# Attention block in float32: scores in half tiles on two single PSUM banks, four banks for the staggered Strassen products, and the residual sum on VectorE

## The chip, the core and the metric

The kernel runs on one core of a Trainium2 chip. A core has a matmul engine (TensorE, PE in the profile; its weight loads are shown as PEld), VectorE (DVE), ScalarE (ACT), GpSimd (POOL) and SyncE (SP), which here issues nearly all DMAs. Each engine works through its own queue of instructions in order and waits on semaphores of the others. Matmuls write into PSUM, which has eight banks of 128 x 512 float32; VectorE and ScalarE read them, GpSimd can't. The metric is the device time of one execution in microseconds; a lower time is better. Executions of this kernel before agree within 0.1% (3429.11 to 3431.4 us).

## The reference

For each of 16 images x of 512 channels by 1024 positions (all float32):

```python
xn = group_norm(x, 8 groups, eps=1e-5) * gamma + beta
q, k, v = split(qkv_w @ xn + qkv_b, 3)           # 4 heads of 128 channels
attn = softmax(q^T k * 128 ** -0.5, axis=keys)    # per head, 1024 x 1024
out = proj_w @ (v attn^T) + proj_b
return x + out
```

## The kernel before

**Attention.** The loop runs over steps s; a step is one image b, one head h and one block j of 128 keys, so a head has 8 steps (NB) and an image 32. `scores(s)` multiplies the key block with all 1024 queries in two matmuls of 512 into one tile of two banks (pool `ps_s`, two such tiles), takes the exponential of the 1024 columns in one ScalarE instruction (L626) and adds the result to the head's running total on VectorE (L629, L631). `weighted_sum(s)` multiplies values by exponentials into `po`, one tile of two banks (pool `ps_o`) in which all 8 steps of a head accumulate; after the last step ScalarE copies it out in one instruction (L671). `denominators` reduces the total on VectorE and sends the reciprocal through memory to all partitions; `divide` (L674) applies it two steps into the next head. In the program's order a step is: scores of s, then the step's part of the plan, then (at a head's first step) the denominators of the head before, then the weighted sum of s - 1.

**Products with the weights.** Queries, keys, values and the projection are computed by Strassen's method: seven products for a 2 x 2 block product. `strassen` makes seven units of work, in the order of ORDER = 1, 2, 6, 5, 7, 4, 3. A set of units uses two PSUM banks: x holds products 1, 6, 7 and 4, which accumulate on one another, with a copy by ScalarE after each (`kept_copy`, L398, and L496 or L579); y holds product 2, and then, as a new tile, products 5 and 3; VectorE adds the copies to them when it reads them out (L498, L581). Pool `ps_a` has one bank for x and one for y, so a new y must wait until the old one is read.

For queries and keys of two heads (`qk_groups`) and for the projection (`proj_groups`) the method is applied at two levels (`two_levels`): the seven outer products are done in four groups of (1, 5), (2, 6), (7, 4) and (3), and each group runs the seven inner products for its members side by side, with 256 columns each. The first unit of a group (`prepare`) fetches the weights and forms the four inner sums t1 to t4 on VectorE (L468); the last one calls `combine`, which adds up the outer level (L511 to L518) and calls `finish`. For queries and keys `finish` adds the bias (L532); for the projection it loads the residual x into a tile y (SP, L593), adds it on GpSimd to one of the two addends (L602, `eng`), then on VectorE adds bias and the other addend (L603) and stores the result. The values (`v_units`) need one level, in two sets.

**The plan.** While a head's attention runs, its plan puts other work into the eight steps (`plan_head`, `spread`): in h = 0 queries and keys of the image's second pair of heads; in h = 1 the projection of the image before, and the load, statistics and normalisation of the next image; in h = 2 the values of the next image; in h = 3 queries and keys of its first pair. Units of one group follow those of the group before without overlap. For the first image, and for the last image's projection after the loop, there is no attention to run beside: there `staggered` runs two sets against each other, with a lag of 1 or 4 units, and the second set uses a tile of `ps_s` as its two banks (`spare`), other pools' tiles for the sums (`room`) and for one result (`r3`).

The order of instructions on each engine isn't only the program's: a scheduler places instructions at compile time, by the program's order as priority, as soon as its own reckoning has their inputs ready and their tiles free, and it assigns PSUM and SBUF buffers. In the trace the halves of a weighted sum stand between products. What an engine does at run time follows that fixed order.

Of the kernel before, what the change touches and what calls it, by code (L numbers as in the profile page):

```python
# [16 lines left out]
P = 128  # L17
# [130 lines left out]
def fast_path(ctx, tc, x, sources, out, consts, flag, dims):  # L148
# [30 lines left out]
    ps_a = ctx.enter_context(tc.tile_pool(name="ps_a", bufs=1, space=PSUM))  # L179
# [202 lines left out]
    def strassen(name, mm, out_, spare=False, width=HALF):  # L382
# [4 lines left out]
        def bank(which):  # L387
            if spare:
                if "both" not in t:
                    t["both"] = ps_s.tile([P, N], F32, tag="s", name=f"{name}_spare")  # L390
                return t["both"][:, ts("xy".index(which), HALF)]
            return ps_a.tile([P, HALF], F32, tag=which, name=f"{name}_{which}")
# [41 lines left out]
    def two_levels(name, site, b, blocks, finish, spare=(), room=None, r3=None):  # L434

# [8 lines left out]
        def group_units(g):  # L444
# [4 lines left out]
            def prepare():  # L449
                have["w"] = group_weights(site, g, b == 0 and site != "proj")  # L450
                if g == 3:
                    R[g] = r3() if r3 else rpool.tile(
                        [P, 2, 2, HALF], F32, tag="r0", name=f"{name}_r3"
                    )
                else:
                    R[g] = rpool.tile([P, 2, 2, HALF], F32, tag=f"r{g}", name=f"{name}_r{g}")
                sums = ("t1", "t2", "t3", "t4")
                if g in spare:
                    for m, t in zip(sums, room(f"{name}_{g}")):
                        have[m] = t.rearrange("p (i q) -> p i q", q=Q)  # L460
                else:
                    for m in sums:
                        have[m] = tpool.tile(
                            [P, 2, Q], F32, tag=f"in_{m}", name=f"{name}_{g}_{m}"
                        )
                for i, p in enumerate(group):
                    def put(o, a, c):
                        nc.vector.tensor_sub(have[o][:, i, :], inner(i, a), inner(i, c))  # L468
                    put("t1", "b12", "b11")
                    put("t2", "b22", "t1")  # L470
                    put("t3", "t2", "b11")
                    put("t4", "b21", "t2")
# [27 lines left out]
            units = strassen(f"{name}_{g}", mm, out_, g in spare, n * Q)  # L500
            first = units[0]
# [250 lines left out]
    def run(units):  # L752
        for u in units:
            u()
# [188 lines left out]
```

## Time and profile before

| What | Value |
|---|---|
| median of 3 runs | 3430.12 us |
| the profiled execution, and its span | 3429.16 us, 3427.4 us |
| before the first score matmul | 70.5 us |
| after the last weighted sum | 50.0 us |
| PE, PEld, DVE, ACT, POOL busy | 96%, 58%, 72%, 34%, 6% |
| granted TensorE clock, mean | 0.994 |
| DMA | 104 GB/s over the span |

A profile shows one execution. Busy time is what an engine spent in instructions; matmul rows are pipelined, and their ends are modelled, so that the distance between two starts says more than a busy share. In a row of a timeline stand the start, the length, the engine, the line, the operation, the tiles (result <- inputs) and the number of instructions merged; in brackets the idle time ahead of it and what ended it. In a row of the view of waits stand the waiting and the awaited instruction, then the total in us, how many times, and the longest.

### The profile page before, as it was taken

To read this page: it belongs to the slowest core of one execution; us is meant where nothing else is said; L and a number is where in the kernel's file an instruction comes from. 1 tells how busy PE (TensorE), PEld (TensorE's weight loads), DVE (VectorE), ACT (ScalarE), POOL (GpSimd) and SP (SyncE) were. 2 spreads that over 40 slices of the span, in tenths; PEclk is the share of its full clock that TensorE was granted. 3 is DMA by queue.
4 is the path that set the end of the run, shared out by engine and by line. 5 is a ranking of instruction groups with operands and counts; after the bars stand their busy time and mean duration, and the time that the engine had idled before them with its cause. 6 is when DMAs were issued, how large, how long until landed. Compare 5 with 4: busy or idle time off the path is not lost.

```text
span 3427.4 us, 30729 instructions
## 1 busy us (share of the span) xinstructions
PE 3282.7 (96%) x10708; PEld 1985.4 (58%) x10708; DVE 2473.8 (72%) x4305; ACT 1172.2 (34%) x1602; POOL 190.9 (6%) x140
## 2 busy tenths in 40 slices
PE   7999999999999999999999999999999999999997
PEld 6565555655556555565555656555565555655654
DVE  8858577675776858668586785867758677586776
ACT  2423334233333333333333333333333333333332
POOL 0000101000010000101001010010100101001010
PEclk9999999999999999999999999999999999999998
DMA  5323333233332333333233332323323233233232
GB/s 167 127 77 123 104 102 104 93 109 102 101 111 88 110 111 108 106 103 109 85 109 107 107 111 81 119 92 109 116 74 119 95 109 118 76 112 111 81 109 79
DMA packets 114018, 357.37 MB, mean 104 GB/s; under 512 B 15424, under 2 KB 27200, under 8 KB 113856
## 3 DMA queue, kind: packets, MB, share of 16 engines
q1 hardware_dynamic: 112848, 354.27, 30.8%
q8 instruction: 87, 1.43, 0.2%
q10 hardware_dynamic: 1008, 1.06, 0.1%
q14 instruction: 75, 0.61, 0.1%
HBM read 310.00 MB, written 45.29 MB: 104 GB/s over the span
## 4 chain that ended last, share of the span: by engine, by line
PE 70%; DVE 12%; DMA 11%; ACT 3%; issue 2%; POOL 2%; SPq 1%; POOLq 0%; ACTq 0%; DVEq 0%
PE po L665 19%; PE s L621 18%; PE qk_x L483 9%; PE qk_y L483 7%; PE v_x L561 5%; PE pp_x L483 4%; PE v_y L561 4%; DMA rinv<-row 3%; DMA w_v<-kept_v 3%; PE pp_y L483 3%; DVE y L603 2%; DVE tot L631 2%; POOL pp_r L602 2%; ACT x L232 1%; DMA y<-in_x 1%
## 5 line engine op out<-in xcount | busy, mean ns | idle before, releaser
L665 PE MATMUL po<-p,v 128*128 128x512 f32 x2048 | 1018.7, 593 | 15.0 <-ACT o L671 15.0
L626 ACT ACTIVATE p<-s 128x1024 f32<-128x1024 f32 x512 | 523.5, 1023 | 1364.7 <-PE s L621 1285.2
L621 PE MATMUL s<-qk,qk 128*128 128x512 f32 x2048 | 979.7, 596 | 0.0
L631 DVE TENSOR_TENSOR tot<-tot,p 128x1024 f32<-128x1024 f32 x384 | 468.4, 1220 | 365.0 <-ACT p L626 363.4
L621 PEld LDWEIGHTS s<-qk,qk 128*128 128x128 f32 x2048 | 387.3, 191 | 376.0 <-issue 355.1
L665 PEld LDWEIGHTS po<-p,v 128*128 128x128 f32 x2048 | 387.5, 190 | 162.9 <-issue 100.4
L483 PE MATMUL qk_x<-qk_t,w 128*128 128x256 f32 x1326 | 364.6, 391 | 0.3 <-ACT qk_u L398 0.3
L483 PEld LDWEIGHTS qk_x<-qk_t,w 128*128 128x128 f32 x1326 | 238.3, 189 | 176.0 <-ACT qk_u L398 79.3
L602 POOL TENSOR_TENSOR pp_r<-pp_r,y 128x512 f32<-128x512 f32 x120 | 173.0, 1451 | 2927.0 <-ACT pp_r L496 2686.4
L498 DVE TENSOR_TENSOR qk_r<-qk_y,qk_u 128x512 f32<-128x512 f32 x252 | 156.0, 619 | 46.0 <-PE qk_y L483 45.8
L398 ACT COPY qk_u<-qk_x 128x512 f32<-128x512 f32 x252 | 133.8, 531 | 154.3 <-PE qk_x L483 153.7
L483 PE MATMUL pp_x<-pp_t,w_proj 128*128 128x256 f32 x654 | 181.8, 395 | 0.0
L561 PE MATMUL v_y<-w_v,x 128*128 128x256 f32 x720 | 172.4, 379 | 0.0
L561 PE MATMUL v_x<-w_v,xt 128*128 128x256 f32 x720 | 171.4, 381 | 0.0
L483 PEld LDWEIGHTS pp_x<-pp_t,w_proj 128*128 128x128 f32 x654 | 115.8, 190 | 90.8 <-ACT pp_u L398 38.2
L561 PEld LDWEIGHTS v_y<-w_v,x 128*128 128x128 f32 x720 | 136.7, 190 | 49.8 <-issue 28.1
L561 PEld LDWEIGHTS v_x<-w_v,xt 128*128 128x128 f32 x720 | 135.6, 190 | 40.7 <-issue 14.8
L483 PE MATMUL qk_y<-x,w 128*128 128x256 f32 x504 | 143.8, 387 | 15.3 <-DVE qk_r L498 14.5
L483 PEld LDWEIGHTS qk_y<-x,w 128*128 128x128 f32 x504 | 90.7, 189 | 88.5 <-DVE qk_r L498 68.0
L532 DVE SCALAR_TENSOR_TENSOR qk<-qk_r,qkb_sb,qk_r 128x512 f32<-128x512 f32 x190 | 136.3, 746 | 1.1
L483 PE MATMUL qk_y<-qk_t,w 128*128 128x256 f32 x442 | 122.6, 394 | 3.1 <-DVE qk_r L498 3.1
L483 PEld LDWEIGHTS qk_y<-qk_t,w 128*128 128x128 f32 x442 | 78.8, 189 | 77.2 <-DVE qk_r L498 57.4
(202 smaller groups left out, 3523.5 us busy)
## 6 DMA issues: line engine op xcount, KB each, us to landing
w<-kept SPq DMA_DIRECT2D x90, 896.0 KB, 4.7
w_v<-kept_v SPq DMA_DIRECT2D x60, 768.0 KB, 4.4
w_proj<-kept_proj SPq DMA_DIRECT2D x48, 896.0 KB, 4.7
rinv<-row SPq DMA_DIRECT2D x64, 512.0 KB, 3.7
y<-in_x SPq DMA_DIRECT2D x128, 256.0 KB, 3.6
out_y<-y SPq DMA_DIRECT2D x128, 256.0 KB, 2.3
x<-in_x SPq DMA_DIRECT2D x62, 512.0 KB, 4.1
w<-kept SPq DMA_DIRECT2D x30, 448.0 KB, 3.3
```

Of the source, the lines that this page charges most:

```text
L232: nc.scalar.activation(t, t, AF.Identity, bias=beta_sb[:, i], scale=sc[:, i])
L398: nc.scalar.copy(t[n][:, :width], t["x"][:, :width])
L483: nc.tensor.matmul(acc[:, ts(i, Q)], have["w"][:, i, SLOTS[an], :], inner(i, bn), start=(first and i == 0), stop=True, skip_group_check=True,)
L498: nc.vector.tensor_add(dst, view(a), view(c))
L532: nc.vector.scalar_tensor_tensor(st[b, h][:, ts(half, HALF)], a[:, r, :], qkb_sb[:, i : i + 1], c[:, r, :], ALU.add, ALU.add,)
L561: nc.tensor.matmul(acc[:, ts(g, HC)], xb[b][bn][k][:, ts(2 * jj + g, P)], wi[:, k, :], start=(first and g == 0 and k == 0), stop=(k == KC ...
L602: eng.tensor_add(c[:, r, :], c[:, r, :], t)
L603: nc.vector.scalar_tensor_tensor(t, a[:, r, :], projb_sb[:, o : o + 1], c[:, r, :], ALU.add, ALU.add)
L621: nc.tensor.matmul(sc[:, ts(half, HALF)], ks[b, h][:, ts(j, P)], qs[b, h][:, ts(half, HALF)], start=True, stop=True,)
L626: nc.scalar.activation(ps[s], sc, AF.Exp, scale=SCALE)
L631: nc.vector.tensor_add(tot[b, h], tot[b, h], ps[s])
L665: nc.tensor.matmul(po[b, h][:, ts(half, HALF)], vs[b, h // 2][:, h % 2, j, :], p[:, ts(half, HALF)], start=(j == 0), stop=(j == NB - 1),)
```

## The change

PSUM has eight banks in both. Before: two tiles of two banks for scores, one of two for `po`, one bank each for x and y. After: two tiles of one bank for scores, one of two for `po`, two banks each for x and y.

- `scores` and `weighted_sum` take a half as argument. A step is now: (at a head's first step) denominators of the head before; then for each half of 512 queries the scores of s with their exponential, the weighted sum of s - 1, and half of the step's part of the plan. The total is added after the second half, in one instruction as before. `po` is copied out in halves.
- The groups of units are always staggered: group g starts at position 0, 4, 8 or 14 (0, 4, 10 for three groups), in the plan as well as in prologue and tail. `spare`, `room` and `r3` are gone.
- `prepare` is taken apart: weights, t1 and t2 come with product 1, t3 with product 2, t4 with product 6. The result tiles of a group take turns in three buffers (g % 3).
- The residual is added on VectorE, in the other order: bias, first addend and residual in one instruction, then the second addend.
- The load of the next image, its statistics and its normalisation come one step earlier in h = 1.

```diff
-    ps_a = ctx.enter_context(tc.tile_pool(name="ps_a", bufs=1, space=PSUM))
+    ps_a = ctx.enter_context(tc.tile_pool(name="ps_a", bufs=2, space=PSUM))
...
-            def prepare():
+            def weights():
+                R[g] = rpool.tile([P, 2, 2, HALF], F32, tag=f"r{g % 3}", name=f"{name}_r{g}")
                 have["w"] = group_weights(site, g, b == 0 and site != "proj")
...
+            def inner_sum(m):
+                have[m] = tpool.tile([P, 2, Q], F32, tag=f"in_{m}", name=f"{name}_{g}_{m}")
+                a, c = {
+                    "t1": ("b12", "b11"), "t2": ("b22", "t1"), "t3": ("t2", "b11"),
+                    "t4": ("b21", "t2"),
+                }[m]
+                for i in range(n):
+                    nc.vector.tensor_sub(have[m][:, i, :], inner(i, a), inner(i, c))
...
-            units = strassen(f"{name}_{g}", mm, out_, g in spare, n * Q)
-            first = units[0]
-            units[0] = lambda: (prepare(), first())
-            last = units[-1]
-            units[-1] = lambda: (last(), combine(g))
-            return units
+            p1, p2, p6, p5, p7, p4, p3 = strassen(f"{name}_{g}", mm, out_, n * Q)
+            return [
+                lambda: (weights(), inner_sum("t1"), inner_sum("t2"), p1()),
+                lambda: (inner_sum("t3"), p2()), lambda: (inner_sum("t4"), p6()),
+                p5, p7, p4, lambda: (p3(), combine(g)),
+            ]
...
-                eng.tensor_add(c[:, r, :], c[:, r, :], t)
                 nc.vector.scalar_tensor_tensor(
-                    t, a[:, r, :], projb_sb[:, o : o + 1], c[:, r, :], ALU.add, ALU.add
+                    t, a[:, r, :], projb_sb[:, o : o + 1], t, ALU.add, ALU.add
                 )
+                nc.vector.tensor_add(t, t, c[:, r, :])
...
-    def scores(s):
+    def scores(s, half):
         b, h, j = where(s)
-        sc = ps_s.tile([P, N], F32, tag="s", name=f"s_{s}")
-        for half in range(NH2):
-            nc.tensor.matmul(
-                sc[:, ts(half, HALF)], ks[b, h][:, ts(j, P)], qs[b, h][:, ts(half, HALF)],
-                start=True, stop=True,
-            )
-        ps[s] = ppool.tile([P, N], F32, tag="p", name=f"p_{s}")
-        nc.scalar.activation(ps[s], sc, AF.Exp, scale=SCALE)
+        sc = ps_s.tile([P, HALF], F32, tag="s", name=f"s_{s}_{half}")
+        nc.tensor.matmul(
+            sc, ks[b, h][:, ts(j, P)], qs[b, h][:, ts(half, HALF)], start=True, stop=True
+        )
+        if half == 0:
+            ps[s] = ppool.tile([P, N], F32, tag="p", name=f"p_{s}")
+        nc.scalar.activation(ps[s][:, ts(half, HALF)], sc, AF.Exp, scale=SCALE)
+        if half == 0 or j == 0:
+            return
...
         if j == NB - 1:
-            os_[b, h] = opool.tile([P, N], F32, tag="o", name=f"o_{b}_{h}")
-            last_eviction[b] = nc.scalar.copy(os_[b, h], po.pop((b, h)))
+            if half == 0:
+                os_[b, h] = opool.tile([P, N], F32, tag="o", name=f"o_{b}_{h}")
+            last_eviction[b] = nc.scalar.copy(os_[b, h][:, i], po[b, h][:, i])
...
+    def staggered(lists):
+        starts = (0, 4, 8, 14)[: len(lists)] if len(lists) != 3 else (0, 4, 10)
+        at = [(a + i, g, u) for g, (a, us) in enumerate(zip(starts, lists))
+              for i, u in enumerate(us)]
+        return [u for _, _, u in sorted(at, key=lambda t: t[:2])]
...
-            spread(plan, sum(qk_groups(b, 1), []), 0, NB)
+            spread(plan, staggered(qk_groups(b, 1)), 0, NB)
...
-                plan[1].append(lambda: load_x(b + 1))
-                spread(plan, [lambda c=c: stats_chunk(b + 1, c) for c in range(NCC)], 3, 7)
-                plan[6].append(lambda: stats_group(b + 1))
-                plan[7] += [lambda c=c: normalise(b + 1, c) for c in range(NCC)]
+                plan[0].append(lambda: load_x(b + 1))
+                spread(plan, [lambda c=c: stats_chunk(b + 1, c) for c in range(NCC)], 2, 6)
+                plan[5].append(lambda: stats_group(b + 1))
+                plan[6] += [lambda c=c: normalise(b + 1, c) for c in range(NCC)]
...
-    run(staggered([v_units(0, 0), v_units(0, 1, spare=True)], 1))
+    run(staggered([v_units(0, 0), v_units(0, 1)]))
     stage_sums(0)
-    run(staggered(
-        qk_groups(0, 0, spare=(1, 3), room=room(opool, "o"), r3=r3(opool, "o")), 4
-    ))
+    run(staggered(qk_groups(0, 0)))
...
     for s in range(steps + 1):
+        units = []
         if s < steps:
             b, h, j = where(s)
             if j == 0:
                 plan = plan_head(b, h)
-            scores(s)
-            if j == 2 and s > NB:
-                divide(*where(s - NB)[:2])
-            run(plan[j])
+            units = plan[j]
+        if s > 0 and s % NB == 0:
+            denominators(*where(s - 1)[:2])
+        for half in range(NH2):
+            if s < steps:
+                scores(s, half)
+                if half == 0 and j == 2 and s > NB:
+                    divide(*where(s - NB)[:2])
+            if s > 0:
+                weighted_sum(s - 1, half)
+            n = (len(units) + 1) // 2
+            run(units[half * n : (half + 1) * n])
...
-    run(staggered(groups[1:], 4))
+    run(staggered(groups[1:]))
```

More of the change, by code (lines that the diff above doesn't have):

```diff
@@ L379, in v_sums, with strassen @@
             nc.sync.dma_start(store["v"][:, i], wv[FACTORS[p][0]])
-    def strassen(name, mm, out_, spare=False, width=HALF):
+    def strassen(name, mm, out_, width=HALF):
         t = {}
         def bank(which):
[L388 to L391, printed above, removed]
             return ps_a.tile([P, HALF], F32, tag=which, name=f"{name}_{which}")
@@ L535, in finish, with v_units @@
                 )
[L537 to L539 removed]
+        return two_levels(f"qk_{b}_{pair}", pair, b, lambda: xb[b], finish)
+    def v_units(b, jj):
         w = {}
@@ L805, in fast_path @@
     o_blocks(last)
-    groups = proj_groups(last, nc.vector, spare=(1, 3), room=room(qkpool, "qk1"), r3=r3(qkpool, "qk0"))
+    groups = proj_groups(last)
     sums_of_b(ob[last], (1,))
```

78 lines of the change are left out of this document (19 added, 59 removed).

## The prediction

> **What bounds the kernel now.** The page first: which engine fills the span.
>
> ```profile
> PE 3282.7 (96%) x10708; PEld 1985.4 (58%) x10708; DVE 2473.8 (72%) x4305; ACT 1172.2 (34%) x1602; POOL 190.9 (6%) x140
> ```
>
> TensorE (PE) looks full, but matmul ends are modelled, so I measure it by starts. The timeline, for a stretch of bare attention and for one with products:
>
> ```profile
> 3357.24 1.88 PE L665 MATMUL po<-p,v 128*128 128x512 f32 x4
> 3358.96 1.88 PE L621 MATMUL s<-qk,qk 128*128 128x512 f32 x4
> ...
> 1246.24 1.89 PE L561 MATMUL v_y<-w_v,x 128*128 128x256 f32 x8
> 1247.96 1.89 PE L561 MATMUL v_x<-w_v,xt 128*128 128x256 f32 x8
> ```
>
> Four passes of 512 columns start 1.72 us apart: 0.43 us each (an f32 product is two passes). Eight of 256 columns: 0.215 us each. A group of four is shown 1.88 long although the next starts after 1.72, so a wait shorter than about 0.17 us shows no idle time. The table by windows, first for the body of the kernel, then head by head for one image (h = 0, 1, 2, 3):
>
> ```profile
> 70.50:3377.40 3306.90, 3197.92 (x10378) 1920.24 (x10377) 2385.27 (x4121) 1143.86 (x1552) 189.20 (x135) 1.00 0.31 103
> ...
> 1104.20:1155.60 51.40, 50.34 (x164) 30.06 (x163) 43.59 (x79) 17.06 (x25) 0.00 (x0) 1.00 0.37 125
> 1155.60:1208.90 53.30, 50.29 (x163) 29.81 (x162) 44.88 (x73) 16.96 (x25) 9.15 (x7) 1.00 0.37 127
> 1208.90:1265.20 56.30, 53.52 (x182) 33.40 (x181) 29.38 (x51) 22.34 (x25) 3.21 (x3) 1.00 0.26 84
> 1265.20:1314.90 49.70, 49.70 (x163) 29.92 (x162) 35.40 (x63) 16.96 (x25) 0.00 (x0) 1.00 0.24 79
> ```
>
> The columns are length, busy time of PE, PEld, DVE, ACT, POOL, then the granted clock (1.00 all through). The body holds 4096 passes of 512 (64 heads of 64) and 10378 - 4096 = 6282 small ones: 4096 x 0.43 + 6282 x 0.215 = 3112 us of pure streaming in 3307, so **about 195 us are gaps**. By head the floor is 64 x 0.43 + 98 x 0.215 = 48.6 us (51.6 in h = 2 with 112 small passes), so the gaps are 2.8, 4.7, 4.7 and 1.1 us. VectorE (DVE) has 44.9 us of work in the head that takes 53.3. Who ends TensorE's waits, from the view of waits:
>
> ```profile
> PE pp_y L483 <- DVE pp_r L498: 44.8, 32, 1.9
> PE qk_y L483 <- DVE qk_r L498: 18.6, 40, 1.4
> PE po L665 <- ACT o L671: 15.0, 14, 1.1
> PE v_x L561 <- ACT x L232: 14.8, 28, 0.6
> PE pv L60 <- DVE vv L58: 12.0, 15, 1.2
> ...
> PE v_x L561 <- DMA w_v<-kept_v: 3.9, 12, 0.4
> ```
>
> They sum to 109.1 us in 141 waits; with 0.17 hidden in each, 133 of the 195. The other 62 are waits too short to show. The longest kind, seen in PE's and DVE's timelines of h = 1:
>
> ```profile
> 1184.62 1.03 PE L483 MATMUL pp_y<-ot,w_proj 128*128 128x256 f32 x4
> 1185.51 1.13 PE L483 MATMUL pp_x<-pp_t,w_proj 128*128 128x256 f32 x4
> 1186.48 1.88 PE L665 MATMUL po<-p,v 128*128 128x512 f32 x4
> 1190.26 1.13 PE L483 MATMUL pp_y<-pp_t,w_proj 128*128 128x256 f32 x4 [1.89 <-DVE pp_r L498]
> ...
> 1186.58 0.75 DVE L603 SCALAR_TENSOR_TENSOR y<-pp_r,projb_sb,pp_r 128x512 f32<-128x512 f32 x1 [1.16 <-POOL pp_r L602]
> 1187.25 1.22 DVE L631 TENSOR_TENSOR tot<-tot,p 128x1024 f32<-128x1024 f32 x1
> 1188.38 1.22 DVE L512 TENSOR_TENSOR pp_r<-pp_r,pp_r 128x1024 f32<-128x1024 f32 x1
> 1189.52 0.68 DVE L498 TENSOR_TENSOR pp_r<-pp_y,pp_p 128x512 f32<-128x512 f32 x1
> ```
>
> Product 2 wrote bank y at 1184.62; its reader on DVE stands behind a wait for POOL and two long additions and runs at 1189.52; product 5 needs the same single bank and stands still until 1190.26.
>
> **The change part by part.** Each term is for the whole run.
>
> *Two y and two x banks, groups staggered.* Product 5 now opens the other y bank, whose last reader belongs to product 3 of the group before, one product and at least one pair of half scores and sums (1.72 us) earlier. c11's reader, late above, no longer holds the next product. The two y rows are 63.4 us plus 72 x 0.17 = 75.6. Bounds: all of it gone, or none where DVE is late for the other bank too. I take three quarters, nearest to the trace's case, in which only the c11 bank was late: **-57**. The rest of the gaps (62) are mostly x copies and sums that come just in time; the staggering puts another group's product between them in the middle of a list, not at its first four and last eight products. Bounds +20 to -62; I take a third: **-20**.
>
> *Halves of scores.* The matmuls stay the same in number. ScalarE (ACT) pays more starts:
>
> ```profile
> L626 ACT ACTIVATE p<-s 128x1024 f32<-128x1024 f32 x512 | 523.5, 1023 | 1364.7 <-PE s L621 1285.2 <-DVE worst L655 68.6 <-DVE ot L253 8.4
> L671 ACT COPY o<-po 128x1024 f32<-128x1024 f32 x64 | 64.4, 1007 | 96.3 <-PE po L665 96.3
> L398 ACT COPY pp_u<-pp_x 128x512 f32<-128x512 f32 x94 | 54.8, 583 | 59.8 <-PE pp_x L483 58.8 <-DVE pp_room L468 1.1
> ```
>
> A copy of half the width saves 424 ns, so half an exponential is about 599 and two cost 175 more: 512 x 0.175 = 90 us, and 64 x 0.159 = 10 for the halved evictions. ACT goes from 34% to 37% and waits 1285 us for scores, which hides it. A score bank is needed again a full step later (3.43 us at the least, in bare attention, of which 0.86 is its own matmul) against 0.6 of exponential: cost **0**; without that cover it would be the 100 us.
>
> *Eviction of po in halves.* The first half is copied beside the second half's matmuls; the next head's sums come after a half score. The 15.0 us row plus 14 x 0.17 = 17.4; bounds 0 (the next head's tile still waits for both halves) to all. The copy left is 0.58 us against 0.86 of scores: **-17**.
>
> *Statistics a step earlier.* The x loads, sums and normalisation of the next image (4 chunks in two ACT passes) move up one step, about 6.5 us, where the waits for x are at most 0.6 us. 14.8 + 28 x 0.17 = 19.6, all gone: **-20**. Their loads go past the projection's loads on SP, which then wait behind the release of x. The pv wait I leave at **0**: it is the latency of a short DVE chain, wherever it stands. The w_v row stays too.
>
> *Residual on VectorE.*
>
> ```profile
> L602 POOL TENSOR_TENSOR pp_r<-pp_r,y 128x512 f32<-128x512 f32 x120 | 173.0, 1451 | 2927.0 <-ACT pp_r L496 2686.4 <-DMA y<-in_x 173.0 <-DVE tt L638 34.9
> L602 DVE TENSOR_TENSOR pp_r<-pp_r,y 128x512 f32<-128x512 f32 x6 | 4.0, 685 | 0.3 <-ACT pp_r L496 0.2
> L514 DVE TENSOR_TENSOR pp_r<-pp_r,pp_r 128x1024 f32<-128x1024 f32 x16 | 36.0, 2251 | 1.6
> L514 DVE TENSOR_TENSOR qk_r<-qk_r,qk_r 128x1024 f32<-128x1024 f32 x32 | 39.2, 1225 | 3.1
> L603 DVE SCALAR_TENSOR_TENSOR y<-pp_r,projb_sb,pp_r 128x512 f32<-128x512 f32 x94 | 83.4, 902 | 25.8 <-POOL pp_r L602 25.7
> L603 DVE SCALAR_TENSOR_TENSOR y<-pp_r,projb_sb 128x512 f32<-128x512 f32 x32 | 22.6, 748 | 1.4
> L468 DVE TENSOR_TENSOR pp_t<-ot,pp_t 128x256 f32<-128x256 f32 x94 | 52.9, 576 | 0.0
> L468 DVE TENSOR_TENSOR qk_t<-xt,qk_t 128x256 f32<-128x256 f32 x190 | 76.3, 416 | 0.0
> ```
>
> DVE takes 120 x 0.685 = 82 us more. The same DVE operations are longer beside POOL's additions than elsewhere: 16 x 1.026 + 94 x 0.154 + 94 x 0.160 = 46 us, which go. Net +36 us, 2.4 per image, in the head that has 44.9 of 48.6 filled: 47.3. The slack almost goes; I let a third reach TensorE: **+12** (bounds -26, the end of the waits for POOL, to +36).
>
> The Trainium skill ("SBUF — State Buffer", the section on the two separate sides) says that VectorE and GpSimd share one port pair as an exclusive lock. The trace agrees in kind (2251 against 1225 ns); by that rule each of POOL's additions could block up to its own 1451 ns, an estimate of 174 us freed where the rows give 46, and the term would be below zero.
>
> *Prologue and tail.* They lose the spare banks and buffers, but two bank sets remain; only the wider lags (0, 4, 10) and single buffers for sums are new. **+2**, bounds -5 to +10.
>
> Sum: -57 - 20 - 17 - 20 + 12 + 2 = **-100**. The profiled execution took 3429.16 us (span 3427.4), the median is 3430.12; so 3430 - 100 = **3330**, its own range 3285 to 3370.
>
> **The rivals.** *DVE's order stays the bound:* the other bank's reader is late just as often, since DVE is about 90% full in h = 0 and 1 (43.6 and 44.9 of 48.6). For it: the 1189.52 row waited for other DVE work, not for data. Against: h = 3, at 35.4 us of DVE, has hardly a gap. Then y -19, short waits -5, the rest as above: -47, **3383**.
>
> *Slower: the denominators go first.* Their chain is now issued ahead of the next head's scores and sums. In the trace it is mixed with other work:
>
> ```profile
> 1262.53 1.25 DVE L638 STREAM_TRANSPOSE tt<-tot 128x1024 f32<-128x1024 f32 x1
> ...
> 1264.94 0.68 DVE L581 TENSOR_TENSOR v<-v_y,v_u 128x512 f32<-128x512 f32 x1
> ...
> 1267.01 0.07 DVE L655 DVE_READ_ACCUMULATOR worst<-l,r 32x1 f32 x1
> ```
>
> From 1262.53 to 1267.08 less 0.68 it is 3.87 us in one block, and product 6 of the head's first group waits for the sums behind it. In the 48 heads with staggered groups that is at most 186 us: 3330 + 186 = **3516**; from 2.1 us uncovered per head it eats the gain. Against: the first products need no sums, and 5.2 us of scores, sums and products come before product 6.
>
> *The wait for y moves to DVE.* POOL's 173.0 us behind the loads of y would stop DVE's queue, with the readers of both banks behind it: at most **3503**. Against: the loads land well before DVE uses them:
>
> ```profile
> 1191.41 1.26 POOL L602 TENSOR_TENSOR pp_r<-pp_r,y 128x512 f32<-128x512 f32 x1 [4.87 <-DMA y<-in_x]
> ...
> 1201.11 1.42 DVE L603 SCALAR_TENSOR_TENSOR y<-pp_r,projb_sb 128x512 f32<-128x512 f32 x2
> ```
>
> The Trainium skill ("TensorE: Matmul & The Clock Gate", table at its head) has VectorE's queue as strict FIFO; by that rule whatever waits there holds all behind it.
>
> *Nearly all gaps go:* -195 + 14, **3249**.
>
> **How the numbers follow.** Forecast 0.58, DVE's order 0.20, denominators 0.11, y on DVE 0.03, all gaps 0.08. A difference of 0.2% (7 us) is about what a measurement of this kernel can tell from none. Faster: 0.58 + 0.08 + 0.16 of the first rival = 0.82; same 0.03; slower 0.15. The range 3262 to 3412 leaves out the two slower rivals and the edge of the last.
>
> **What would show it.** Right: h = 2 near 53 us, h = 1 near 51, no wait of po for o, the two y rows under 25 us together, DVE near 2510 busy, ACT near 1270. Wrong: PE waiting on DVE at the first product 6 of a head (denominators), DVE waiting on DMA y, or y rows as long as before.

## The result and the profile after

The changed kernel takes **3250.57 us** (median of 4 runs, 3249.11 to 3251.55), against 3430.76 for the kernel before on the same chip: ratio **0.9472**, 95% interval 0.9455 to 0.9488. That is 180 us less, where 100 was forecast: below the range (3262 to 3412) and within 2 us of the rival in which nearly all gaps go (3249).

Lines of the kernel after that the rows below name: L603 scores, L608 their exponential, L615 the total, L648 weighted sum, L658 divide; L466 and L545 the products for projection, queries and keys and for the values, L394 and L479 ScalarE's copies of x, L481 VectorE's reading of y, L585 and L588 the two instructions of the residual, L49 to L62 the group statistics (pm, d, vv, pv), L232 the second pass of the normalisation. e6, e10 and e15 have the lines of before.

The page of the kernel after, busy time of each engine:

```profile
PE 3202.9 (99%) x10708; PEld 2011.9 (62%) x10708; DVE 2476.6 (76%) x4425; ACT 1290.0 (40%) x2178; POOL 16.8 (1%) x20
```

Its table by windows, the body (first score to last weighted sum), then h = 0 to 3 of the image shown in the prediction; length, busy time of PE, PEld, DVE, ACT, POOL, granted clock, DMA:

```profile
67.00:3200.70 3133.70, 3126.34 (x10386) 1951.51 (x10386) 2390.62 (x4246) 1262.76 (x2131) 15.12 (x15) 1.00 0.32 108
...
1050.80:1099.70 48.90, 48.90 (x164) 30.67 (x163) 43.04 (x78) 19.15 (x34) 0.00 (x0) 1.00 0.38 131
1099.70:1148.00 48.30, 48.30 (x163) 30.19 (x162) 42.43 (x79) 22.52 (x37) 0.00 (x0) 1.00 0.39 133
1148.00:1201.60 53.60, 53.33 (x182) 33.82 (x181) 28.70 (x50) 19.88 (x31) 1.01 (x1) 1.00 0.28 94
1201.60:1250.30 48.70, 48.70 (x163) 30.69 (x163) 38.15 (x68) 19.14 (x34) 0.00 (x0) 1.00 0.24 81
```

The span went from 3427.4 to 3247.3. Of the 180.1 us between them the body gave 173.2 (3306.9 to 3133.7), the prologue 3.5 (70.5 to 67.0), the tail 3.4 (50.0 to 46.6). By the prediction's own floor, 3112 us of streaming, 22 us of gaps are left in the body of the 195 before. The four heads took 51.4, 53.3, 56.3 and 49.7 us; now 48.9, 48.3, 53.6 and 48.7 against floors of 48.6, 48.6, 51.6 and 48.6 (work moves a little between heads, hence a head under its floor).

The view of waits, TensorE's own, of the kernel after:

```profile
PE pm L49 <- DVE mean L47: 11.8, 1, 11.8
PE pp_y L466 <- DVE pp_r L481: 5.4, 2, 5.1
PE pp_y L466 <- DVE o L658: 5.0, 1, 5.0
PE v_y L545 <- ACT x L232: 3.8, 14, 0.3
PE s L603 <- DVE qk L516: 1.3, 1, 1.3
```

The first row is the start of the kernel, the next two stand in the tail. In the body hardly a wait is left: the y rows (44.8 and 18.6), the wait of po for its copy (15.0) and that of pv (12.0) have gone, and the values' wait for x has fallen from 14.8 to 3.8.

### The profile page after: what moved, and what is told of

The parts are those of the page before. It is cut to its first block, busy times and chain, and to the rows that moved or that the text cites. A ratio compares the mean times of both kernels' runs of the same rounds, so it can differ in the third digit from the quotient of the medians.

```text
span 3247.3 us, 31121 instructions
## 1 busy us (share of the span) xinstructions
PE 3202.9 (99%) x10708; PEld 2011.9 (62%) x10708; DVE 2476.6 (76%) x4425; ACT 1290.0 (40%) x2178; POOL 16.8 (1%) x20
## 4 chain that ended last, share of the span: by engine, by line
PE 90%; ACT 5%; DVE 3%; DMA 1%; issue 1%; POOL 0%; ACTq 0%; SPq 0%; POOLq 0%; DVEq 0%
PE s L603 25%; PE po L648 25%; PE qk_x L466 12%; PE qk_y L466 9%; PE v_x L545 6%; PE v_y L545 5%; PE pp_x L466 5%; PE pp_y L466 3%; ACT x L232 2%; ACT x L231 2%; DVE tot L615 1%; ACT p L608 1%; DVE pp_r L498 1%; POOL rstd L64 0%; DVE pp_r L481 0%
## 5 line engine op out<-in xcount | busy, mean ns | idle before, releaser
L603 PE MATMUL s<-qk,qk 128*128 128x512 f32 x2048 | 1048.4, 593 | 2.2 <-DVE qk L516 1.3
L648 PE MATMUL po<-p,v 128*128 128x512 f32 x2048 | 1045.3, 593 | 0.7 <-ACT p L608 0.7
L608 ACT ACTIVATE p<-s 128x512 f32<-128x512 f32 x1024 | 611.2, 597 | 1053.2 <-PE s L603 1046.4
L615 DVE TENSOR_TENSOR tot<-tot,p 128x1024 f32<-128x1024 f32 x384 | 468.8, 1221 | 315.3 <-ACT p L608 312.1
L648 PEld LDWEIGHTS po<-p,v 128*128 128x128 f32 x2048 | 387.1, 190 | 455.0 <-issue 431.0
L603 PEld LDWEIGHTS s<-qk,qk 128*128 128x128 f32 x2048 | 386.2, 190 | 93.7 <-issue 37.3
L466 PEld LDWEIGHTS qk_x<-qk_t,w 128*128 128x128 f32 x1344 | 250.6, 190 | 199.4 <-issue 140.2
L466 PE MATMUL qk_x<-qk_t,w 128*128 128x256 f32 x1344 | 358.0, 383 | 1.4 <-ACT qk_u L394 1.1
L394 ACT COPY qk_u<-qk_x 128x512 f32<-128x512 f32 (+1 forms) x256 | 136.4, 533 | 240.6 <-PE qk_x L466 239.5
L466 PE MATMUL pp_x<-pp_t,w_proj 128*128 128x256 f32 x672 | 180.3, 385 | 1.1 <-ACT pp_u L394 1.1
L545 PE MATMUL v_y<-w_v,x 128*128 128x256 f32 x720 | 176.5, 381 | 3.8 <-ACT x L232 3.8
L545 PEld LDWEIGHTS v_y<-w_v,x 128*128 128x128 f32 x720 | 135.3, 190 | 66.3 <-issue 40.2
L481 DVE TENSOR_TENSOR qk_r<-qk_y,qk_u 128x512 f32<-128x512 f32 (+1 forms) x256 | 158.4, 619 | 22.8 <-PE qk_y L466 21.4
L466 PEld LDWEIGHTS pp_x<-pp_t,w_proj 128*128 128x128 f32 x672 | 125.1, 191 | 78.1 <-issue 51.7
L545 PEld LDWEIGHTS v_x<-w_v,xt 128*128 128x128 f32 x720 | 136.8, 190 | 57.0 <-issue 43.0
L545 PE MATMUL v_x<-w_v,xt 128*128 128x256 f32 x720 | 170.1, 379 | 0.0
L466 PE MATMUL qk_y<-x,w 128*128 128x256 f32 x512 | 141.8, 379 | 0.0
L394 ACT COPY pp_u<-pp_x 128x512 f32<-128x512 f32 (+1 forms) x128 | 68.2, 533 | 170.0 <-PE pp_x L466 166.9
L565 DVE TENSOR_TENSOR v<-v_y,v_u 128x512 f32<-128x512 f32 x64 | 43.7, 682 | 114.4 <-ACT v_u L394 69.9
L481 DVE TENSOR_TENSOR qk_r<-qk_y,qk_p 128x512 f32<-128x512 f32 (+1 forms) x128 | 79.1, 618 | 57.1 <-PE qk_y L466 57.1
L466 PEld LDWEIGHTS qk_y<-x,w 128*128 128x128 f32 x512 | 97.3, 190 | 39.7 <-issue 21.8
```

What stands on the lines that cost most here:

```text
L394: nc.scalar.copy(t[n][:, :width], t["x"][:, :width])
L466: nc.tensor.matmul(acc[:, ts(i, Q)], have["w"][:, i, SLOTS[an], :], inner(i, bn), start=(first and i == 0), stop=True, skip_group_check=True,)
L481: nc.vector.tensor_add(dst, view(a), view(c))
L545: nc.tensor.matmul(acc[:, ts(g, HC)], xb[b][bn][k][:, ts(2 * jj + g, P)], wi[:, k, :], start=(first and g == 0 and k == 0), stop=(k == KC ...
L565: nc.vector.tensor_add(dst, view(a), view(c))
L603: nc.tensor.matmul(sc, ks[b, h][:, ts(j, P)], qs[b, h][:, ts(half, HALF)], start=True, stop=True)
```

## The experiments

Every kernel was run beside the kernel before, whose median was 3430.8 to 3435.8 from chip to chip; so the ratios are what compares best. "After" and "before" name the two kernels. Three questions: what carried the gain of the residual, what that of the statistics, and what is left for banks and order.

### The residual: GpSimd's additions

**e5: after, residual on GpSimd again** (in the tail on VectorE, as in before).

```diff
-  scalar_tensor_tensor(t, a, projb, t, ADD, ADD);  vector.tensor_add(t, t, c)
+  gpsimd.tensor_add(c, c, t);  scalar_tensor_tensor(t, a, projb, c, ADD, ADD)
```

> The changed kernel with the residual added on GpSimd again (in the tail on VectorE), in the old order of the two additions. If the residual's move costs VectorE time that TensorE feels (the prediction's +12), this is faster: about 3240 us. If the move is a gain (the wait for GpSimd and its port gone), slower: 3270 to 3310 us. If two banks make it indifferent: within 5 us of 3250.

Measured: 3307.67 us, ratio 0.9638 (0.9622 to 0.9654): **57 us of the gain go**. TensorE's waits in this kernel:

```profile
PE pp_x L466 <- ACT pp_p L394: 25.2, 14, 2.0
PE pp_y L466 <- DVE pp_r L481: 19.4, 16, 1.4
```

Both are waits of the projection, about one each in an image, although there are two banks a side. In one image (PE at 1162.55), the copy that the first row waits for stands in ScalarE's queue behind a normalisation step; that waits 2.92 us for a value of VectorE's, and this stands behind an addition of 128x1024 that takes 2.32 us beside GpSimd, where others of its shape take 1.22. So the two banks don't absorb what GpSimd does to VectorE's queue.

**e6: before, with nothing but the residual on VectorE** (the edit of e5 the other way round).

```diff
-  eng.tensor_add(c, c, t);  scalar_tensor_tensor(t, a, projb, c, ADD, ADD)
+  scalar_tensor_tensor(t, a, projb, t, ADD, ADD);  vector.tensor_add(t, t, c)
```

> The kernel before with only the residual on VectorE in its new order. Run e1 is some 90 us below the kernel before without any second bank. If the residual is what gave that (h = 1 lost most of its gaps): 3360 to 3390 us. If the alternation of halves gave it: 3430 within 15 us.

Measured: 3357.01, ratio **0.9777** (0.9761 to 0.9794). One edit that adds 82 us of work to VectorE takes 76 us off the kernel (by the ratio). Its waits:

```profile
PE qk_y L483 <- DVE qk_r L498: 19.8, 40, 2.1
PE po L665 <- ACT p L626: 15.2, 14, 1.1
...
PE pv L60 <- DVE vv L58: 0.8, 1, 0.8
...
PE pp_y L483 <- DVE pp_r L498: 0.3, 2, 0.2
```

With one bank for y the projection's row falls from 44.8 to 0.3 us, and that of pv from 12.0 to 0.8; the row of queries and keys, where GpSimd isn't at work, stays (18.6 to 19.8). The costliest wait of the kernel before was GpSimd's doing, not the bank's. And VectorE's busy time, from the page:

```profile
PE 3271.2 (97%) x10708; PEld 1987.2 (59%) x10708; DVE 2465.6 (73%) x4425; ACT 1170.2 (35%) x1602; POOL 17.7 (1%) x20
```

It does 82 us more and is busy 8.2 us *less* (2473.8 before): by this count some 90 us of contention (VectorE instructions that take longer while GpSimd works) went. The rows of one shape that got shorter in e6 add up to 70 us; the other 20 stand in no row, and neighbouring VectorE instructions overlap a little (two additions of 0.685 take 1.29 together), so 70 is the safer figure. The prediction counted 46 in three groups of rows. It overlooked others of the same kind, such as these two of before (groups by line; total, mean ns), beside 412 and 417 ns for the same shapes in e6:

```profile
L468 DVE TENSOR_TENSOR pp_t<-o,pp_t 128x256 f32<-128x256 f32 x124 | 64.4, 520 | 1.0
...
L468 DVE TENSOR_TENSOR pp_t<-o 128x256 f32<-128x256 f32 x62 | 32.6, 528 | 20.8 <-PE pp_y L483 20.0 <-PE qk_y L483 0.8
```

**e9: after, with only the last of the two additions on GpSimd**, so that VectorE never waits for GpSimd.

```diff
-  vector.tensor_add(t, t, c)
+  gpsimd.tensor_add(t, t, c)      # the last image: vector
```

> The changed kernel with bias, first addend and residual on VectorE, and only the last addition on GpSimd (in the tail on VectorE), so that VectorE never waits for GpSimd but shares its port with it. If e5's loss of 57 us was VectorE's wait for GpSimd: within 8 us of 3250. If it was the longer VectorE operations beside GpSimd's: 3285 to 3310 us, with the additions of 1024 columns near 2.2 us again.

Measured: 3314.23, ratio 0.9652 (0.9636 to 0.9668), 64 us slower than after. One wait of TensorE holds three quarters of it, pv for vv, 48.7 us in 15; most of the rest is a lower clock (mean granted 0.992, against 0.997 in after: an estimate of 17 us). The timeline in one image (VectorE, then GpSimd, then TensorE):

```profile
1157.56 0.15 DVE L54 TENSOR_TENSOR d<-mean,mu 128x4 f32<-128x4 f32 x1
...
1157.70 4.77 DVE L585 SCALAR_TENSOR_TENSOR y<-pp_r,projb_sb,y 128x512 f32<-128x512 f32 x4
1162.39 1.22 DVE L56 TENSOR_TENSOR d<-d 128x4 f32<-128x4 f32 x1
1163.65 1.18 DVE L58 TENSOR_TENSOR vv<-d,mv 128x4 f32<-128x4 f32 x1
...
1158.58 6.24 POOL L588 TENSOR_TENSOR y<-y,pp_r 128x512 f32<-128x512 f32 x4 [9.91 <-issue]
...
1156.01 0.28 PE L49 MATMUL pm<-mean,avg 128*128 128x4 f32 x2
...
1164.98 0.36 PE L60 MATMUL pv<-vv,avg 128*128 128x4 f32 x2 [3.42 <-DVE vv L58]
```

and the same place in after:

```profile
1140.18 0.15 DVE L54 TENSOR_TENSOR d<-mean,mu 128x4 f32<-128x4 f32 x1
...
1145.39 0.15 DVE L56 TENSOR_TENSOR d<-d 128x4 f32<-128x4 f32 x1
...
1146.60 0.15 DVE L58 TENSOR_TENSOR vv<-d,mv 128x4 f32<-128x4 f32 x1
...
1138.62 0.28 PE L49 MATMUL pm<-mean,avg 128*128 128x4 f32 x2
...
1147.00 0.28 PE L60 MATMUL pv<-vv,avg 128*128 128x4 f32 x2
```

An addition of four columns takes 0.15 us alone and 1.2 us while GpSimd adds 512 columns: eight times as long, for no work of its own. TensorE's queue is in order, so everything behind pv stands still. Contention isn't all of this wait, though. From the first `d` to the end of `vv` e9 takes 7.3 us and after 6.6, with four additions of the residual more on VectorE; but in after pv comes 8.4 us behind pm in TensorE's order, filled with other products, and in e9 only some 5.5 us of products stand between them. That would fit an order fixed at compile time by a reckoning that sees less work on VectorE and no contention, which is not shown; e14, with VectorE's work as in after, has 8.6 us between them. The Trainium skill ("SBUF — State Buffer", the section on the two separate sides) calls the shared port pair an exclusive lock that is held for the whole instruction; the 0.15 and 1.2 us agree.

**e14: after, with an addition on GpSimd on which nothing depends.** It overwrites an addend that nobody reads any more, 120 times, and VectorE keeps all of the residual.

```diff
   vector.tensor_add(t, t, c)
+  gpsimd.tensor_add(c, c, a)      # not for the last image
```

> The changed kernel with one more addition on GpSimd for each half row of the residual (120 of 128x512, as many as the kernel before has), written into a tile that nobody reads any more. VectorE never waits for them. Theory: GpSimd holds the port that it shares with VectorE, so VectorE's operations beside it get longer (a 128x1024 addition from 1.22 to over 2 us, a 128x4 one from 0.15 to over 1 us) and TensorE stands behind them: 3290 to 3320, as in e9. Rival: in e9 it was the chain sum, GpSimd, store that cost: 3247 to 3260.

Measured: **3331.46**, ratio 0.9698 (0.9682 to 0.9715): 81 us slower, somewhat more than expected, perhaps because here VectorE's own work isn't reduced. The timeline (VectorE, GpSimd, TensorE):

```profile
1162.21 0.15 DVE L54 TENSOR_TENSOR d<-mean,mu 128x4 f32<-128x4 f32 x1
...
1169.46 1.22 DVE L56 TENSOR_TENSOR d<-d 128x4 f32<-128x4 f32 x1
...
1171.73 1.21 DVE L58 TENSOR_TENSOR vv<-d,mv 128x4 f32<-128x4 f32 x1
...
1169.01 3.92 POOL L590 TENSOR_TENSOR pp_r<-pp_r,pp_r 128x512 f32<-128x512 f32 x2 [1.23 <-DVE y L588]
...
1173.09 0.36 PE L60 MATMUL pv<-vv,avg 128*128 128x4 f32 x2 [3.87 <-DVE vv L58]
```

From `d` to the end of `vv` it is 10.7 us here and 6.6 in after, with the order of TensorE as long (8.6 and 8.4). So contention is enough: work on GpSimd whose result no instruction uses brings the loss back. (Only the release of the addend's buffer comes later. Engines wait for that 5.0 us in the whole run, so it isn't the price.) The wait of pv holds 55.1 of the 81 us, in 15; the lower clock (0.988) gives about the rest, an estimate of 29 us.

### The statistics a step earlier

**e8: after, load, sums, group statistics and normalisation at the steps of before.**

```diff
-  plan[0] load; chunks in steps 2-5; plan[5] stats_group; plan[6] normalise
+  plan[1] load; chunks in steps 3-6; plan[6] stats_group; plan[7] normalise
```

> The changed kernel with the load, statistics and normalisation of the next image at their old steps. The prediction's term: the waits for x (about 20 us) return, 3265 to 3275 us. If the two banks (the statistics' matmuls use a y bank) already took them away: 3250 within 5 us.

Measured: 3324.95, ratio 0.9686 (0.967 to 0.9702): **74 us**, where the prediction had 20 for this term.

**e11: after, with the load, sums and group statistics at the steps of before, the normalisation a step earlier.** The text below speaks of the group statistics as early too; in the kernel that ran they are in step 6, as in e8, so that the normalisation alone is earlier.

```diff
-  plan[0] load; chunks in steps 2-5; plan[5] stats_group; plan[6] normalise
+  plan[1] load; chunks in steps 3-6; plan[6] stats_group; plan[6] normalise
```

> The changed kernel with load and sums of the next image at their old steps, and only the group statistics and the normalisation at the earlier ones. In every trace the means are ready some 37 us before h = 2, and TensorE's first matmul of the statistics stands where the plan puts it. If that place decides: 3250 within 5 us; if load and sums do: 3325 us as in e8.

Measured: 3324.94, ratio 0.9679 (0.9662 to 0.9695), the same as e8. So the place of the normalisation doesn't matter as long as the group statistics come in step 6. What the group statistics bring in step 5 behind late sums wasn't run.

**e13: after, with only the group statistics at the step of before.**

```diff
-  plan[5].append(lambda: stats_group(b + 1))
+  plan[6].append(lambda: stats_group(b + 1))
```

> The changed kernel; only the group statistics (the two small matmuls pm and pv and VectorE's chain between them) go back to the step in which the kernel before has them; load, sums and normalisation stay a step earlier. Theory: TensorE's queue is in order, and what costs is where pm and pv stand in it, so nearly all of the 74 us of e8 come back: 3310 to 3330, with the idle time in h = 2, ahead of the first products for the values. Rival: the earlier load and sums carry the gain: 3245 to 3270.

Measured: 3326.16, ratio 0.9684 (0.9668 to 0.97): this one line is worth all of it. The waits:

```profile
PE v_x L545 <- ACT x L232: 52.0, 26, 3.3
...
PE pv L60 <- DVE vv L58: 7.6, 15, 1.4
```

The products for the values wait for the normalised x, which waits for pv. With the group statistics in step 6 it makes no difference whether the load and the sums come late (e8) or early (e13): TensorE's order holds pm and pv where the plan puts them.

The 52.0 and 7.6 us aren't yet 75. The clock gives about the rest. e8 in one image, as timeline and as windows (granted clock is the third number from the end):

```profile
1174.97 0.39 PE L60 MATMUL pv<-vv,avg 128*128 128x4 f32 x2 [0.47 <-DVE vv L58]
1178.64 0.70 PE L545 MATMUL v_x<-w_v,x 128*128 128x256 f32 x2 [3.28 <-ACT x L232]
```

```profile
1175.00:1179.00 4.00, 0.72 (x4) 0.57 (x4) 3.07 (x6) 2.46 (x3) 1.32 (x1) 1.00 0.59 225
1179.70:1183.00 3.30, 3.23 (x8) 2.60 (x9) 3.15 (x10) 3.30 (x5) 0.00 (x0) 0.51 0.00 0
1183.00:1187.00 4.00, 4.00 (x15) 2.58 (x14) 4.00 (x11) 2.76 (x6) 0.00 (x0) 1.00 0.40 125
```

After the 3.28 us of waiting TensorE runs 3.3 us at half speed: 1.6 us more. The same views show a lower clock at this place in 14 images, so an estimate of 22 us; the mean granted clock, 0.989 in e13 and 0.997 in after, gives 26 of 3324.

**e10: before, with only the statistics a step earlier** (the edit of e8 the other way round).

```diff
-  plan[1] load; chunks in steps 3-6; plan[6] stats_group; plan[7] normalise
+  plan[0] load; chunks in steps 2-5; plan[5] stats_group; plan[6] normalise
```

> The kernel before with only the load, statistics and normalisation one step earlier. The prediction's term by itself: 3410 us. If the statistics' matmuls can't use the earlier place because the single y bank is taken (e1 kept 4.7 us of gaps per image in h = 2): 3430 within 10 us.

Measured: 3437.21, ratio 1.0008 (0.9997 to 1.0019): **nothing** in time. The waits:

```profile
PE po L665 <- ACT p L626: 37.7, 14, 2.8
PE pp_y L483 <- DVE pp_r L498: 29.7, 17, 1.9
...
PE pv L60 <- DVE vv L58: 11.0, 15, 0.8
```

The waits of the values for x are all but gone, the wait of po for its copy too, and pp_y has fallen from 44.8 to 29.7; but pv waits nearly as before (12.0 there), and a new wait of po for an exponential has taken the place of what went. In one image (PE at 1213.93) ScalarE's normalisation stands right ahead of that exponential, and the clock is lower after the wait, 0.65 over 4 us:

```profile
1213.93:1217.93 4.00, 4.00 (x8) 2.35 (x9) 3.77 (x5) 3.54 (x5) 0.01 (x1) 0.65 0.00 0
```

Over the run the granted clock is 0.988, against 0.994 before: an estimate of up to 21 us, which hides what the shorter waits may have won.

**e15: before, with residual on VectorE and statistics a step earlier** (the diffs of e6 and e10).

> The kernel before with two parts of the change, the residual on VectorE (alone 3357) and the statistics a step earlier (alone 3437, six slower than before). Theory: the early pm and pv pay as soon as VectorE's chain between them is no longer held up by GpSimd, which adds the residual in the same steps: 3305 to 3335, with the wait of pv gone. Rival: the early statistics need the two banks a side, since pm and pv each take a y bank from the products: 3350 to 3365.

Measured: **3324.5**, ratio 0.9676 (0.966 to 0.9692), 1.0% below e6. The wait of po for the exponential (15.2 in e6) and that of the values for x (9.7 in e6) are gone. So the early statistics need no second bank; they pay once the residual is off GpSimd. Whether through contention alone isn't shown, since the order on TensorE changes with it: in 14 of the 16 images pv comes 9.8 us behind pm in e15 and 6.8 in e10.

### Banks, order and halves

**e1: after, one bank for x and one for y, groups in sequence.**

```diff
-  ps_a ... bufs=2        staggered: sorted(at, ...)
+  ps_a ... bufs=1        staggered: sum(lists, [])
```

> The changed kernel with one bank each for x and y and the groups in sequence, so that halves of scores, the earlier statistics and the residual on VectorE are left. Theory (banks): the gaps came from a late reader of a single bank; they return, and what stays is the o, x and pv waits of the kernel before (about 17 + 20 + 15 us): about 3380 us, with the two y rows near 60 us. Rival (fill): it is the alternation of half scores and half sums with pairs of products that covers every wait, whatever the banks: 3290 us or less.

Measured: 3342.05, ratio 0.9736 (0.972 to 0.9753), between the two forecasts. The y rows are back, at 35 us instead of near 60:

```profile
PE pp_y L466 <- DVE pp_r L481: 27.4, 34, 3.6
...
PE qk_y L466 <- DVE qk_r L481: 7.6, 16, 1.0
```

**e2: after, two banks for x, one for y, staggered.**

```diff
-  ps_a ... bufs=2      tile(tag=which)
+  ps_a ... bufs=1      tile(tag=which, bufs=2 if which == "x" else 1)
```

> The changed kernel, staggered, with two x banks and one y bank. Banks: product 5 waits again for the reader of product 2, and now for the other group's y as well: the y waits are back at 76 us or more, 3325 us or above. Fill: within 10 us of 3250.

Measured: 3326.71, ratio 0.969 (0.9674 to 0.9706). The second y bank is worth **76 us** in after, as much as the bound in the prediction. About half of it shows as waits of TensorE (37 us more than in after); as the clock is the same (0.997), the rest presumably lies in gaps too short for the view. The groups are still staggered here, so this may hold what staggering costs with a single y bank.

**e3: after, two banks each, groups in sequence.**

```diff
-  staggered: sorted(at, ...)
+  staggered: sum(lists, [])
```

> The changed kernel with two banks each, groups in sequence. Banks: the y waits stay gone, but x copies and sums are just in time again, so that at most the short waits (62 us) return: 3265 to 3310 us. Fill: within 10 us of 3250. A theory by which only the staggering matters expects 3370 us.

Measured: 3262.05, ratio 0.95 (0.9484 to 0.9516). Against e1 the banks bring 80 us; against after the staggering brings 11.5, with intervals that just touch (0.9484 and 0.9488).

**e4: after, with a step in the old order**: both half scores, the plan, both half sums.

```diff
-  for each half: scores(s, half); weighted_sum(s - 1, half); half of the units
+  scores(s, 0); scores(s, 1); units; weighted_sum(s - 1, 0); weighted_sum(s - 1, 1)
```

> The changed kernel with the step in the old order: both half scores, the step's whole part of the plan, both half sums. Banks: the fillers still exist, within 20 us of 3250. Fill: the pairs of products lose their cover, 3320 us or above.

Measured: 3282.81, ratio 0.9561 (0.9545 to 0.9577). The alternation in half steps is worth 32 us. None of it shows in the view of waits (31 us in all, 34 in after), so which gaps it closes stays open.

**e7: after without banks, staggering, residual and statistics** (the diffs of e1, e5 and e8 together): what is left are the halves, the order within a step and the late inner sums.

> The changed kernel with single banks, groups in sequence, residual on GpSimd and the statistics at their old place: only halves, their alternation with the plan, the halved eviction and the denominators' new place are left. If the alternation gave e1's gain: 3340 to 3360 us. If the residual did: about 3400 us, and e1 minus this is what the residual and the statistics add.

Measured: 3441.7, ratio 1.0024 (1.0014 to 1.0034). Alone the halves bring nothing (8 us slower), and po's 15.0 us did go, but to others, and to a lower clock (0.984, against 0.994 before: an estimate of 34 us):

```profile
PE pp_y L466 <- DVE pp_r L481: 42.4, 35, 2.1
PE v_x L545 <- ACT x L232: 41.2, 16, 2.9
PE pv L60 <- DVE vv L58: 24.4, 15, 2.0
```

**e17: after, po copied out whole.**

```diff
-  each half: scalar.copy(os[:, half], po[:, half])
+  after the second half: scalar.copy(os, po)
```

> The changed kernel; po is copied out in one instruction of 1024 columns after the second half's sum, as in the kernel before. By the prediction's term the wait of po for its copy comes back: 17 more, 3265 to 3270. Rival: the next head's first sum stands behind a half score and half of the plan's units, at least 1.3 us, against a copy of 1.0 us: 3248 to 3256.

Measured: 3249.35, ratio 0.9454 (0.9436 to 0.9472): no difference. The wait of po for its copy doesn't come back; TensorE waits for exponentials instead, 8.3 us in 15 where after has 0.9, which the time doesn't show.

**e16: after, denominators behind the step's scores, sums and units.**

```diff
-  denominators(s - 1); for each half: scores, weighted sum, units
+  for each half: scores, weighted sum, units; denominators(s - 1)
```

> The changed kernel; only the denominators of the head before go behind both half scores, sums and the plan's units of a head's first step. If the rival of the prediction were at work, this would be faster, up to some 3.9 us a head, 3245 at most. Theory: TensorE has no wait there, and VectorE's chain is as long wherever it stands; only the divide, two steps later, comes closer to it: 3248 to 3258.

Measured: 3250.34, ratio 0.9458 (0.944 to 0.9475): no difference.

### A version that goes further

**e12: after, with the statistics yet a step earlier and a fourth buffer in the tail.** In the tail of after, the copy of the last group (outer product 3) waits for the result buffer that it shares with an earlier group, VectorE's readings of y for it stand behind the same buffer's last reader, and TensorE waits for these:

```profile
3235.50 0.37 ACT L479 COPY pp_r<-pp_x 128x256 f32<-128x256 f32 x1 [5.01 <-DVE y L588]
...
3236.33 1.22 PE L466 MATMUL pp_y<-o,w_proj 128*128 128x256 f32 x2 [5.08 <-DVE pp_r L481]
```

```diff
+  chunks in steps 1-3; plan[4] stats_group; plan[5] normalise
+  last image: R[3] = qkpool.tile(tag="qk0")      # not r0 again
```

> The changed kernel with statistics and normalisation yet a step earlier, and in the tail a result buffer of its own for group 3, whose copy waited 5.0 us there for the buffer's last reader. If the place of the statistics is what h = 2 still waits for (1.1 us of gaps per image): 3250 - 14 - 4 = 3232 us; if not, 3246 us; if VectorE in h = 1 is too full for them, slower than 3250.

Measured: **3245.65** (3244.02 to 3246.38), ratio 0.9447 (0.9432 to 0.9463). Its median is 5 us below that of after, which was timed in another session; the intervals of the two ratios touch (0.9455 to 0.9463), so that a gain of 0.15 to 0.3% is likely but not settled. Both waits at which it aimed are gone from TensorE's view, the one in the tail and the 3.8 us of the values for x.

## Why the prediction was off, point by point

Along one path through the experiments, starting from before, by ratios times 3430.8: residual on VectorE -76 (e6), statistics earlier -35 (e15), everything else -70 (after). The prediction had +12, -20 and -92 for the same three. **The step that failed is the residual on VectorE**: it is off by 88 us, and the others together by 7 the other way. (Another order of the steps shares the gain out otherwise; undone from after, the residual is worth 57 and the statistics 75, so that their term, -20, is the second that failed.) The signs that the prediction named point there too: h = 2 (53.6 us), the y rows, po and ScalarE came out as forecast, but h = 1, the residual's head, fell to 48.3, not 51, and VectorE is busy 2476.6, not near 2510.

- *Residual, +12.* The step summed VectorE's work (82 - 46 = +36) and asked how full that makes the head. Both halves were wrong. The contention was 70 to 90 us, so that VectorE isn't fuller at all. And the loss wasn't one of load: it is a latency, a short chain or a late reader that gets longer just where TensorE's order stands behind it. The trace of before had it in the fence shown: L603 waiting 1.16 us for POOL, two additions ahead of the late reader of y. By undoing it in after the price is 57 (e5), 64 (e9) or, with VectorE's work kept, 81 us (e14). The rule of the Trainium skill ("SBUF — State Buffer", the section on the two separate sides) that the prediction set aside had the sign right; its estimate of 174 us freed was too much, the 46 of the rows too little (e6: 70 to 90).
- *Second y bank, -57.* The sign and about the size are right for after (76 by e2, the bound), but by luck, since the reason was wrong: most of the 63.4 us of y rows on which it rested belonged to GpSimd (44.8 to 0.3 in e6, with one bank). That the bank earns its 76 us because TensorE, no longer held up elsewhere, comes sooner to the next product is likely but not shown.
- *Short waits by staggering, -20.* 11.5 by e3, little more than can be told from none; the alternation of halves, 32 (e4), had no term of its own.
- *Statistics, -20, pv left at 0.* In after they are worth 75 (e13), in before nothing in time (e10), and there with the residual on VectorE 35 (e15). The term took the waits of before as what there was to win. But the chain from pm to the normalised x has a length of its own; once the other waits go, TensorE reaches the values sooner and meets that chain: "what is late next" was not asked here. And pv's wait isn't the same "wherever it stands": it falls from 12.0 to 0.8 without GpSimd's additions (e6), and in after, which has none, it is 0.8 with the group statistics in step 5 and 7.6 with them in step 6 (e13).
- *Halves of scores, 0.* Right. An exponential of 512 columns takes 597 ns (599 forecast), ScalarE is 1290.0 us busy (near 1270 forecast), and TensorE's waits for it are small, as its rows in after show:

```profile
PE s L603 <- ACT p L608: 0.9, 1, 0.9
...
PE po L648 <- ACT p L608: 0.7, 1, 0.7
...
L608 ACT ACTIVATE p<-s 128x512 f32<-128x512 f32 x1024 | 611.2, 597 | 1053.2 <-PE s L603 1046.4
```

- *po in halves, -17.* The row went, but not by this: with the copy whole it stays away (e17). That the half scores ahead of the next head's first sum cover it is the likely reason; in e17 the longer copy holds up exponentials a little instead (8.3 us).
- *Prologue and tail, +2.* -6.9 in the profile: the prologue gained 3.5 and the tail 3.4.
- *Rivals.* Denominators first: not at work (e16), and in after the waits of products for their inner sums come to 0.2 us. The wait for y on DVE: VectorE waited 1.7 us in all for the loads ahead of L585. VectorE's order as the bound: no, the y rows of the body are gone. Nearly all gaps go: this is what happened, 22 us left, and 0.08 was too small a chance for it.

The parts don't add up one by one: undone singly from after, residual, statistics, y bank, alternation and staggering cost 57 + 75 + 76 + 32 + 12 = 252 us, of 180 gained. Each needs the others, since a queue in order is held by whichever wait is left.

## What to carry to other kernels

Elementwise work moved to GpSimd isn't free for VectorE: look for VectorE operations of one shape with two durations, and for tiny ones that take over 1 us, before believing that the engine with spare time should have the work. Price a late reader by who stands behind it in the queue, not by how full its engine is. And when several waits fall together, ask for each chain that stays (here the statistics) where the faster engine will meet it.

## What the hardware showed that was not expected

- VectorE additions of 128x4 take 0.15 us, and 1.18 to 1.22 us beside a GpSimd addition of 128x512 (e9, e14).
- The clock can fall to half after one wait of a few us in a stream that is otherwise full: 0.51 over 3.3 us after 0.47 and 3.28 us of waiting (e8), and in e14 after 3.87 us, as windows show:

```profile
1173.00:1177.00 4.00, 3.91 (x9) 2.54 (x10) 2.90 (x5) 1.77 (x3) 1.02 (x1) 0.57 0.09 36
1177.00:1181.00 4.00, 4.00 (x16) 2.76 (x15) 3.56 (x6) 4.00 (x5) 0.00 (x0) 1.00 0.15 26
```

It doesn't fall each time. Of 14 waits of 3.41 to 3.43 us in e9, ten were followed by a lower clock within 4 us; four, the image shown among them, left it at 1.00. And shorter waits do it too: in e10 12 of 14 of 2.69 to 2.76 us, in before 3 of 15 of 1.9 us (the row of pp_y). The mean granted clock is 0.988 in e8, e10 and e14, 0.992 in e9 and 0.997 in after. The Trainium skill ("TensorE: Matmul & The Clock Gate", the part on the HAM clock gate) has the clock halved after an idle window of about 3.4 us that runs free of the program. That equal waits sometimes lower the clock and sometimes not agrees with a window that runs free; the falls after 2.69 and 1.9 us don't agree with its length, and here the measurement decides. Where it fell, in e8 and e14, the lower clock cost 1.6 to 1.7 us, about half the wait.
